# Sized transfer lengths in a planner, a second buffer for a reciprocal, and one buffer for norm2 and the output tiles

## The chip, the cores and the metric

The kernel runs on one core of a Trainium2 chip. The metric is the device time of one execution in microseconds. A core has five engines with their own instruction queues: PE (TensorE, matrix products; its weight loads are listed as PEld), DVE (VectorE), ACT (ScalarE), POOL (GpSimd) and SP, which here only issues transfers. Each engine works through its queue in order; semaphores hold an instruction back until what it needs is there.

## What is computed

The reference puts two layers behind each other, for 8 images of 192 channels and 64 x 64 pixels, all in float32.

```python
# layer 0: four scans over the image, one per direction
x = conv1x1(x, W_in)                            # 192 -> 384 channels
x = depthwise 3x3 convolution(x, W_dw) + b_dw
p = conv1x1(x, W_xd)                            # 16 channels
ws, Ls, Us, Ds = (conv1x1(p, w) for w in (W_w, W_l, W_u, W_d))
Gl, Gm, Gr = the three parts of ws, each / (|Gl| + |Gm| + |Gr| + 1e-7)
for 8 steps t:                                  # columns in chunks of 8
    h = l * x + gl * h_up + gm * h + gr * h_down
out = h * Us + xs * Ds                          # x, x transposed, both mirrored
y = sum over the 4 directions with w_m
y = layernorm over channels; global response norm over the image
y = conv1x1(y, W_out)                           # 384 -> 192
# layer 1: attention in windows of 8 x 8, then a two-layer network
s = layernorm(tokens); q, k, v = s @ qkv_w
a = normalised(q) . normalised(k) * temperature # 6 heads of 32
a = where(a >= 16th largest of its row, a, -100) + position bias
x2 = s + (softmax(a) @ v) @ proj_w
x2 = x2 + gelu(layernorm(x2) @ fc1_w) @ fc2_w
```

## The kernel before

Each image goes through three stages. `front` (lines 495 to 610) reads 8 image rows at a time, projects them on PE, writes them with a border to `pad` in HBM, reads strips of four rows back (three transfers for each strip, line 553), convolves them on PE (line 565) and writes the result twice to HBM, as `xs` and `xsT` (lines 598, 599). `scan` (from line 613) makes 8 steps t. A step loads `x0` (line 631), makes the 16-channel proxy `xe`, `xo`, and then 12 tiles of 128 channels x 512 pixels (4 directions x 3 channel tiles), each with a load `xd` for three of the directions (line 694). A tile takes four gate products on PE (line 678), absolute values on ACT (735, 757), products with the state on DVE (742, 744), sums on POOL (766, 781, 785), the sum of the absolute values on DVE (774), then a reciprocal as a logarithm and an exponential on ACT (777, 779) into the tile `rr`; `rr` is multiplied onto the sum on DVE (792) and onto the state products on POOL (796), and DVE makes the new state (800, 807). Pairs of tiles are added to the output `y3` (lines 833 to 855). `norm` (from line 861) normalises `y3` over the channels with the help of two small tiles, `m4` here and `xq` in the proxy, and stores it to `z` in HBM (line 928). `window_row` (from line 1009) treats 8 image rows, that is 8 windows: it loads `zg` (line 1032), scales it (1037), projects to tokens (1052), makes q, k, v (1102, 1141), the attention (1217 to 1332), the projection with the residual into `x2` (1366, 1378), the second norm into `xn` (1421), the network (1453, 1457, gelu 1473, 1487), and writes two output tiles: `ot0` (channels 0 to 127) and `ot1` (the other 64), made on ACT from PSUM (line 1501) and sent by SP (1513, 1516).

The order of all this is not the order of the program. Every operation is handed to a `Plan` as a step: its engine, its estimated cost, what it reads and writes, a rank, and a lane. `Plan.run` makes a list schedule from these estimates: of the steps whose inputs are ready and whose buffers are free by its own account, an engine takes the one of lowest rank, if it needn't idle over 40 ns for it. `Plan.order` does this twelve times with ranks corrected by the last schedule, keeps the shortest by its own estimates, and emits the instructions in that order. The engines then follow it at run time, with semaphores for the true dependences. A step's cost has two parts: how long it holds its engine, and how much later its result is there. For transfers, whose engine is SP, this was `dma(n)`: 350 ns for each of n transfers, and 2600 ns more.

Image b's scan is planned beside the window rows of image b - 1 and the front of image b + 1. So the kernel begins with the front of image 0 alone, then image 0's scan with the front of image 1, and ends with the rows of image 7 alone.

A tile that a `Held` names is made when the plan reaches its first user. Its tag and `bufs` say which buffers it shares and how many there are: the next tile of the tag gets a buffer when all users of an earlier one are done. An entry (tile, "room") makes a step on PE wait, in the plan, for that buffer, though the step itself doesn't write the tile. Before the change `rr` has one buffer, `ot0` shares the one of `xn`, `ot1` has its own, and `m4` and `xq` have one each.

Of the kernel before, what the change touches and what calls it, by code (L numbers as in the profile page):

```python
# [31 lines left out]
P = 128  # L32
B, DM, H, W = 8, 192, 64, 64
DIN, ND, NS = 384, 4, 16
CT = DIN // P
CH = 8
HEADS, HD, WS = 6, 32, 8
# [7 lines left out]
RG = 32  # L45
NEG = -100.0
# [242 lines left out]
def tile_ss2d_then_window_attention(ctx: ExitStack, tc: tile.TileContext, a: dict, out: bass.AP):  # L289
# [6 lines left out]
    nc = tc.nc  # L296
# [47 lines left out]

    ident = blank("ident", [P, P])
    make_identity(nc, ident)
    mean384 = blank("mean384", [P, P], 1.0 / DIN)
    eps5 = blank("eps5", [P, 1], 1e-5)
    eps7 = blank("eps7", [P, 1], 1e-7)
    neg = blank("neg", [P, 64], NEG)  # L350

    hid = [[blank(f"hid{d}_{ct}", [P, (H + 2) * CH], 0.0) for ct in range(CT)] for d in range(ND)]

# [109 lines left out]
    mm = lambda slots, n, share=1.0: (slots * n * 4.0, share)  # L463

    mg = lambda share=1.0: (512 * 5.0 + 240, share)
    dma = lambda n=1: (350.0 * n, 2600.0)
    tiny = (150.0, 90.0)
    log_c = {}
    log_half = blank("log_half", [P, 1], math.log(0.5) / 3)
# [25 lines left out]
    def front(b, xs, xsT):  # L495
        xb = x[b]
        padded = pad[b % 2]

        def read(s):


            def get():
                for k in range(2):
                    rows = slice(8 * (s + k), 8 * (s + k) + 8)
                    nc.sync.dma_start(xt[:, k], xb[0:P, rows, :])
                    nc.sync.dma_start(xt[64 * k : 64 * k + 64, 2], xb[P:DM, rows, :])

            plan("SP", dma(4), get, w=["xt", (xs, "room"), (xsT, "room")])

        def project(ct, s):  # L510

            own = padded[ct * P : (ct + 1) * P]
            cols = slice(ct * P, (ct + 1) * P)
            pins = [bank() for _ in range(2)]

            def products():
                outs = [p().rearrange("p (h w) -> p h w", h=8) for p in pins]
                for k in range(2):
                    nc.tensor.matmul(outs[k], lhsT=w_in[:, 0, cols], rhs=xt[:, k], start=True, stop=False)
                for k in range(2):  # L520
                    half = slice(64 * k, 64 * k + 64)
                    nc.tensor.matmul(outs[k], lhsT=w_in[half, 1, cols], rhs=xt[half, 2], start=False, stop=True)

            plan("PE", mm(3, 512), products, r=["xt"], w=pins)
            for k in range(2):
                cur, pin = xin[k], pins[k]
                plan(
                    "ACT",
                    act(512),
                    lambda cur=cur, pin=pin: nc.scalar.copy(  # L530
                        cur[:, :, 1 : W + 1], pin().rearrange("p (h w) -> p h w", h=8)
                    ),
                    r=[pin],
                    w=[("xin", k)],
                )
                plan(
                    "SP",
                    dma(),
                    lambda cur=cur, row=8 * (s + k) + 1: nc.sync.dma_start(own[:, row : row + 8, :], cur),
                    r=[("xin", k)],  # L540
                    w=[("pad", b % 2, ct, s + k)],
                )

        def convolve(ct, s):

            own = padded[ct * P : (ct + 1) * P]
            pc = bank()
            for k in range(2):
                strip = strips[k]

                def read(row=8 * s + 4 * k, strip=strip):
                    for dy in range(3):
                        nc.sync.dma_start(
                            strip[dy * RG : (dy + 1) * RG],
                            own[:, row + dy : row + dy + 4, :].rearrange("(q m) h w -> m q (h w)", m=RG),
                        )

                near = [("pad", b % 2, ct, n) for n in range(max(0, s + k - 1), min(NG, s + k + 1))]
                plan("SP", dma(3), read, r=near, w=[("strip", k)])
                rows4 = strip.rearrange("p q (h w) -> p q h w", h=4)  # L560

                def products(k=k, rows4=rows4):
                    for dx in range(3):
                        for q in range(4):
                            nc.tensor.matmul(  # L565
                                pc()[q * RG : (q + 1) * RG, k * 256 : (k + 1) * 256].rearrange("p (h w) -> p h w", h=4),
                                lhsT=w_cv[:, ct, q, dx, :],
                                rhs=rows4[:, q, :, dx : dx + W],
                                start=dx == 0,
                                stop=dx == 2,  # L570
                            )
# [16 lines left out]
            sn = Held(fpool, [P, 8, W], "sn")  # L588
            plan(
                "ACT",  # L590
                act(512),
                lambda: nc.scalar.activation(
                    sn(), pc().rearrange("p (h w) -> p h w", h=8), AF.Identity, bias=b_dw[:, ct : ct + 1]
                ),
                r=[pc],
                w=[sn],
            )
            plan("SP", dma(), lambda: nc.sync.dma_start(xs()[:, ct, :, rows], st()), r=[st], w=[(xs, ct, s)])
            plan("SP", dma(), lambda: nc.sync.dma_start(xsT()[:, ct, :, rows], sn()), r=[sn], w=[(xsT, ct, s)])
# [12 lines left out]

    def scan(b, xs, xsT, z, made):
# [14 lines left out]
        def proxy(t):  # L628

            x0 = Held(spool, [P, CT, 512], "x0", bufs=1)  # L630
            plan("SP", dma(), lambda: nc.sync.dma_start(x0(), xs()[:, :, t, :]), r=[xs], w=[x0])
            px = bank()

            def products():
# [47 lines left out]
        def tile_of(t, d, ct, xp, x0, y3, last):  # L682

            ch = d * DIN + ct * P
            if d == 0:
                xd = x0
                flat = lambda: x0()[:, ct, :]
            else:
                xd = Held(spool, [P, 512], "xd", bufs=4)
                src = xs if d == 2 else xsT  # L690
                plan(
                    "SP",
                    dma(),
                    lambda: nc.sync.dma_start(xd(), src()[:, ct, CH - 1 - t if d >= 2 else t, :]),
                    r=[(src, ct, s) for s in range(NG)],
                    w=[xd],
                )
                flat = lambda: xd()
# [71 lines left out]

            def rest():
                if t > 0:
                    rr = Held(spool, [P, 512], "rr", bufs=1)
                    plan("DVE", vec(512), lambda: nc.vector.tensor_add(nb(), nb(), ab()[:, 0, :]), r=[ab], w=[nb])  # L774

                    plan(
# [84 lines left out]
        def norm(t, y3):  # L861
            pm = bank()

            def means(dst, src):

                for ct in range(CT):
                    for q in range(4):
                        nc.tensor.matmul(
                            dst()[RG * q : RG * (q + 1), 0:P],
                            lhsT=mean384[:, 0:RG],  # L870
                            rhs=src()[:, ct, q * P : (q + 1) * P],
                            start=ct == 0,
                            stop=ct == CT - 1,
# [7 lines left out]
                        dst()[:, q * P : (q + 1) * P], lhsT=first, rhs=src(), start=True, stop=True  # L881
                    )

            m4 = Held(spool, [P, P], "m4", bufs=1)
            plan("PE", mm(3, P), lambda: means(pm, y3), r=[y3], w=[pm])
            plan("ACT", act(P), lambda: nc.scalar.copy(m4(), pm()[:, 0:P]), r=[pm], w=[m4])
            plan("PE", mm(4, P), lambda: spread(pm, m4), r=[m4], w=[pm])
# [37 lines left out]
                r=[pv],  # L925
                w=[y3],
            )
            plan("SP", dma(), lambda: nc.sync.dma_start(z()[:, :, t, :], y3()), r=[y3], w=[(z, t)])
            for ct in range(CT):
                plan(  # L930
                    "ACT",
# [52 lines left out]
        def mean_g():  # L984
            for ct in range(CT):
                nc.tensor.matmul(
                    pg()[:, 0:1], lhsT=mean384, rhs=gn()[:, ct : ct + 1], start=ct == 0, stop=ct == CT - 1
                )

        plan("PE", mm(3, 128), mean_g, r=[gn], w=[pg])  # L990
# [18 lines left out]
    def window_row(b, g, z, sc, bb):  # L1009
# [19 lines left out]


        zg = Held(lpool, [P, CT, CH, 64], "zg", bufs=1)
        plan("SP", dma(), lambda: nc.sync.dma_start(zg(), z()[:, :, :, g * 64 : (g + 1) * 64]), r=[z], w=[zg])

        def scaled_up():
            for ct in range(CT):
# [443 lines left out]
        for ci in range(2):  # L1479
            pf = bank()  # L1480
            n = GT // (ci + 1)

            ot = Held(lpool, [P, WS, n // WS], f"ot{ci}", bufs=1, tag="ot1" if ci else "xn")
            def narrowed(ci=ci, pf=pf, n=n):
                def sums(lhsT, rhs, at, k, **flags):
                    dst = pf()[64 * k : 64 * k + 64] if ci else pf()
# [145 lines left out]
```

## Time and profile before

| what | value |
|---|---|
| three runs | 8303.1, 8295.51, 8274.17 us (median 8295.51) |
| profiled execution | 8293.82 us |
| span of its instructions | 8292.0 us |
| mean granted clock of PE | 0.827 |
| busy: PE, DVE, POOL, ACT | 6951.0, 6381.9, 5859.7, 5488.0 us |
| moved by DMA | 695.70 MB, 84 GB/s over the span |
| convolution of the strips (565, PE) | 9216 matmuls, 678.3 us busy |
| logarithm, exponential into rr (777, 779) | 672 each, mean 685 and 633 ns |
| multiplications by rr (792 DVE, 796 POOL) | 672 each, mean 692 and 1298 ns |

Busy time is the time in which an engine executes, as a share of the span. The profile also cuts the span in 40 slices with the busy tenths of each engine. A group of instructions has its busy time, the mean of one, and the idle time of its engine just before it with what ended it ("<-"). A line of the waits names the waiting engine and line, what ended the wait, the total, the number and the longest. The windows view gives the busy times within chosen stretches.

### The profile page before, as it was taken

How to read it: one execution, taken by the hardware profiler on the slowest of the kernel's cores; microseconds unless marked ns; L12 is line 12 of the kernel's file. 1: busy time of each engine (PE TensorE's matmuls, PEld its weight loads, DVE VectorE, ACT ScalarE, POOL GpSimd, SP SyncE). 2: the span in 40 equal slices, each digit the busy share in tenths (PEclk: the TensorE clock that was granted, in tenths of full speed). 3: DMA queues.
4: the chain of work that ended last, by engine and by line, in shares of the span. 5: the costliest groups of instructions: out<-in, count | busy, mean ns of one | idle time of the engine just before them, and what ended most of it. 6: DMA issues, size and time to landing. Idle time of an engine off the chain costs nothing.

```text
span 8292.0 us, 147108 instructions
## 1 busy us (share of the span) xinstructions
PE 6951.0 (84%) x51224; PEld 3600.7 (43%) x51224; DVE 6381.9 (77%) x15421; ACT 5488.0 (66%) x12537; POOL 5859.7 (71%) x5918
## 2 busy tenths in 40 slices
PE   5677688788988898888988898888888789888887
PEld 2333344444444444444444444444444444444454
DVE  1366777888788987888788887888888888888643
ACT  1355346766677666777577766777677676677787
POOL 0377877788778877788778777778788788877411
PEclk8887579788898788888898889888788887778898
DMA  6776146111542135411532126311111112111110
GB/s 175 193 191 180 42 128 165 50 44 45 139 129 74 52 96 138 107 45 56 157 103 77 46 76 171 91 46 46 57 41 50 43 41 66 41 48 41 30 22 15
DMA packets 1037948, 695.70 MB, mean 84 GB/s; under 512 B 704115, under 2 KB 860214, under 8 KB 1037206
## 3 DMA queue, kind: packets, MB, share of 16 engines
q1 hardware_dynamic: 1035830, 684.99, 30.9%
q8 instruction: 407, 6.67, 0.3%
q14 instruction: 335, 2.74, 0.1%
q10 hardware_dynamic: 1376, 1.30, 0.1%
HBM read 453.43 MB, written 232.67 MB: 83 GB/s over the span
## 4 chain that ended last, share of the span: by engine, by line
PE 23%; ACT 15%; DVE 14%; POOL 9%; DMA 5%; issue 4%; SPq 0%; POOLq 0%; DVEq 0%; ACTq 0%
PE g L678 6%; PE lp L1487 3%; PE lp L1453 2%; ACT at L1286 2%; ACT at L1298 2%; DMA zg<-z 2%; POOL pr L796 2%; PE lp L1052 2%; PE lp L565 2%; DVE pr L742 1%; PE lp L1102 1%; POOL pr L781 1%; ACT ab L735 1%; DMA strip<-pad 1%; POOL ab L766 1%
## 5 line engine op out<-in xcount | busy, mean ns | idle before, releaser
L678 PE MATMUL g<-xe,w_g 32*128 32x512 f32 x3648 | 1281.3, 777 | 284.0 <-DVE dx L833 90.3
L678 PE MATMUL g<-xo,w_g 32*128 32x512 f32 x3648 | 1218.2, 767 | 270.1 <-DVE dx L833 154.0
L796 POOL TENSOR_TENSOR pr<-pr,rr 128x512 f32<-128x512 f32 x672 | 872.5, 1298 | 369.4 <-ACT rr L779 320.5
L781 POOL TENSOR_TENSOR pr<-pr 128x512 f32<-128x512 f32 x672 | 887.2, 1321 | 339.7 <-DVE pr L742 254.8
L766 POOL TENSOR_TENSOR ab<-ab 128x512 f32<-128x512 f32 x672 | 873.4, 1300 | 269.6 <-ACT ab L735 264.7
L735 ACT ACTIVATE ab<-g 128x512 f32<-128x512 f32 x1344 | 778.7, 594 | 295.1 <-PE nb L678 175.5
L847 POOL TENSOR_TENSOR dx<-dx,hu 128x512 f32<-128x512 f32 x576 | 738.8, 1294 | 257.6 <-DVE hu L838 250.8
L565 PE MATMUL lp<-strip,w_cv 128*32 128x256 f32 x9216 | 678.3, 438 | 289.0 <-DMA strip<-pad 265.9
L785 POOL TENSOR_TENSOR pr<-pr 128x512 f32<-128x512 f32 x672 | 884.2, 1316 | 20.6
L678 PEld LDWEIGHTS g<-xe,w_g 32*128 32x128 f32 x3648 | 451.9, 219 | 835.0 <-DVE dx L833 206.5
L678 PEld LDWEIGHTS g<-xo,w_g 32*128 32x128 f32 x3648 | 423.4, 217 | 812.4 <-DVE dx L833 278.4
L777 ACT ACTIVATE rr<-nb,eps 128x512 f32<-128x512 f32 x672 | 460.4, 685 | 436.5 <-DVE nb L774 320.8
L1487 PE MATMUL lp<-hd,w_f 128*64 128x256 f32 (+1 forms) x2304 | 610.1, 505 | 63.4 <-ACT hd L1473 39.7
L792 DVE SCALAR_TENSOR_TENSOR nb<-nb,rr 128x512 f32<-128x512 f32 x672 | 464.7, 692 | 237.6 <-ACT rr L779 236.1
L565 PEld LDWEIGHTS lp<-strip,w_cv 128*32 128x32 f32 x9216 | 313.5, 122 | 659.3 <-issue 388.6
L855 POOL TENSOR_TENSOR y<-y,dx 128x512 f32<-128x512 f32 x384 | 593.9, 1555 | 1.8
L800 DVE SCALAR_TENSOR_TENSOR nb<-nb,pr 128x512 f32<-128x512 f32 x672 | 464.4, 691 | 152.5 <-POOL pr L796 148.1
L774 DVE TENSOR_TENSOR nb<-nb,ab 128x512 f32<-128x512 f32 x672 | 464.7, 691 | 128.9 <-POOL ab L766 98.8
L845 POOL TENSOR_TENSOR y<-hu,dx 128x512 f32<-128x512 f32 x192 | 247.3, 1296 | 418.8 <-DVE hu L838 415.7
L757 ACT ACTIVATE nb<-nb 128x512 f32<-128x512 f32 x672 | 397.8, 592 | 206.5 <-DVE pr L742 107.8
L838 DVE TENSOR_TENSOR hu<-g,hid 128x512 f32<-128x512 f32 x768 | 511.4, 678 | 4.6 <-PE g L678 1.7
L678 PE MATMUL nb<-xe,w_g 32*128 32x512 f32 x672 | 506.4, 844 | 8.8 <-DVE hid L807 8.6
(202 smaller groups left out, 17104.4 us busy)
## 6 DMA issues: line engine op xcount, KB each, us to landing
strip<-pad SPq DMA_DIRECT2D x1152, 132.0 KB
xd<-xsT SPq DMA_DIRECT2D x384, 256.0 KB
pad<-xin SPq DMA_DIRECT2D x192, 264.0 KB
xs<-st SPq DMA_DIRECT2D x192, 256.0 KB
xsT<-sn SPq DMA_DIRECT2D x192, 256.0 KB
xd<-xs SPq DMA_DIRECT2D x192, 256.0 KB
x<-xs SPq DMA_DIRECT2D x64, 768.0 KB
z<-y SPq DMA_DIRECT2D x64, 768.0 KB
```

Source lines behind the costliest of these rows:

```text
L565: nc.tensor.matmul(pc()[q * RG : (q + 1) * RG, k * 256 : (k + 1) * 256].rearrange("p (h w) -> p h w", h=4), lhsT=w_cv[:, ct, q, dx, :], rh ...
L678: nc.tensor.matmul(dst, lhsT=w[rows, col : col + P], rhs=xp[rows, :], start=True, stop=True)
L735: lambda r=r: nc.scalar.activation(ab()[:, r, :], g[r](), AF.Abs),
L766: plan("POOL", gp(512), lambda: nc.gpsimd.tensor_add(ab()[:, 0, :], ab()[:, 0, :], ab()[:, 1, :]), w=[ab])
L774: plan("DVE", vec(512), lambda: nc.vector.tensor_add(nb(), nb(), ab()[:, 0, :]), r=[ab], w=[nb])
L781: plan("POOL", gp(512), lambda: nc.gpsimd.tensor_add(one(), one(), pr()[:, 1, :]), r=[(pr, 1)], w=[(pr, 0)])
L785: lambda: nc.gpsimd.tensor_add(one(), one(), pr()[:, 2, :]),
L796: plan("POOL", gp(512), lambda: nc.gpsimd.tensor_mul(one(), one(), rr()), r=[rr], w=[(pr, 0)])
L838: lambda: nc.vector.tensor_mul(like(hu(), d), like(pu(), d), state(d, ct)),
L847: plan("POOL", gp(512), lambda: nc.gpsimd.tensor_add(dx(), dx(), hu()), r=[hu], w=[dx])
L855: nc.gpsimd.tensor_add(y, y, dx().rearrange("p (c i) -> p i c", c=CH))
L1487: nc.tensor.matmul(dst[:, at : at + rhs.shape[-1]], lhsT=lhsT, rhs=rhs, **flags)
```

## The change

Three things are edited. The estimate of a transfer's hold on SP takes its size: `dma(n, kb)` holds for the larger of 350 ns for each transfer and 5.4 ns for each KB of the step; the part for the landing stays at 2600 ns. Ten calls are given their KB; those of the small `flat` and of `xe` stay without. `rr` gets a second buffer. `ot1` moves into the buffer of `xn`, which `ot0` already uses, `m4` moves into that of `xq`, and two constants shrink: `mean384` from 128 to 32 columns, whose first column one small product (line 986) now takes broadcast, and `neg` from 64 columns to one. No instruction of the computation is added or taken away; the planner's order is computed anew.

```diff
-    mean384 = blank("mean384", [P, P], 1.0 / DIN)
+    mean384 = blank("mean384", [P, RG], 1.0 / DIN)
...
-    neg = blank("neg", [P, 64], NEG)
+    neg = blank("neg", [P, 1], NEG)
...
-    dma = lambda n=1: (350.0 * n, 2600.0)
+    dma = lambda n=1, kb=0: (max(350.0 * n, 5.4 * kb), 2600.0)
...
-            plan("SP", dma(4), get, w=["xt", (xs, "room"), (xsT, "room")])
+            plan("SP", dma(4, 786), get, w=["xt", (xs, "room"), (xsT, "room")])
...
-                plan("SP", dma(3), read, r=near, w=[("strip", k)])
+                plan("SP", dma(3, 396), read, r=near, w=[("strip", k)])
...
-            plan("SP", dma(), lambda: nc.sync.dma_start(xs()[:, ct, :, rows], st()), r=[st], w=[(xs, ct, s)])
+            plan("SP", dma(1, 360), lambda: nc.sync.dma_start(xs()[:, ct, :, rows], st()), r=[st], w=[(xs, ct, s)])
...
-            plan("SP", dma(), lambda: nc.sync.dma_start(x0(), xs()[:, :, t, :]), r=[xs], w=[x0])
+            plan("SP", dma(1, 768), lambda: nc.sync.dma_start(x0(), xs()[:, :, t, :]), r=[xs], w=[x0])
...
-                    rr = Held(spool, [P, 512], "rr", bufs=1)
+                    rr = Held(spool, [P, 512], "rr", bufs=2)
...
-            m4 = Held(spool, [P, P], "m4", bufs=1)
+            m4 = Held(spool, [P, P], "m4", tag="xq", bufs=1)
...
-                    pg()[:, 0:1], lhsT=mean384, rhs=gn()[:, ct : ct + 1], start=ct == 0, stop=ct == CT - 1
+                    pg()[:, 0:1], lhsT=mean384[:, 0:1].to_broadcast([P, P]), rhs=gn()[:, ct : ct + 1], start=ct == 0, stop=ct == CT - 1
...
-        plan("SP", dma(), lambda: nc.sync.dma_start(zg(), z()[:, :, :, g * 64 : (g + 1) * 64]), r=[z], w=[zg])
+        plan("SP", dma(1, 900), lambda: nc.sync.dma_start(zg(), z()[:, :, :, g * 64 : (g + 1) * 64]), r=[z], w=[zg])
...
-            ot = Held(lpool, [P, WS, n // WS], f"ot{ci}", bufs=1, tag="ot1" if ci else "xn")
+            ot = Held(lpool, [P, WS, n // WS], f"ot{ci}", bufs=1, tag="xn")
...
-            plan("SP", dma(1 + ci), put, r=[ot], w=[("out", b, g, ci)])
+            plan("SP", dma(1 + ci, 256 >> ci), put, r=[ot], w=[("out", b, g, ci)])
```

The other transfers get their sizes in the same way: the write of `pad` 264, `xsT` 360, `xd` 256, `z` 768.

More of the change, by code (lines that the diff above doesn't have):

```diff
@@ L537, in project @@
                     "SP",
-                    dma(),
+                    dma(1, 264),
                     lambda cur=cur, row=8 * (s + k) + 1: nc.sync.dma_start(own[:, row : row + 8, :], cur),
@@ L597, in convolve @@
             )
-            plan("SP", dma(), lambda: nc.sync.dma_start(xs()[:, ct, :, rows], st()), r=[st], w=[(xs, ct, s)])
-            plan("SP", dma(), lambda: nc.sync.dma_start(xsT()[:, ct, :, rows], sn()), r=[sn], w=[(xsT, ct, s)])
+            plan("SP", dma(1, 360), lambda: nc.sync.dma_start(xs()[:, ct, :, rows], st()), r=[st], w=[(xs, ct, s)])
+            plan("SP", dma(1, 360), lambda: nc.sync.dma_start(xsT()[:, ct, :, rows], sn()), r=[sn], w=[(xsT, ct, s)])
         for s in range(0, NG + 1, 2):
@@ L692, in tile_of @@
                     "SP",
-                    dma(),
+                    dma(1, 256),
                     lambda: nc.sync.dma_start(xd(), src()[:, ct, CH - 1 - t if d >= 2 else t, :]),
@@ L869, in means @@
                             dst()[RG * q : RG * (q + 1), 0:P],
-                            lhsT=mean384[:, 0:RG],
+                            lhsT=mean384,
                             rhs=src()[:, ct, q * P : (q + 1) * P],
@@ L927, in norm @@
             )
-            plan("SP", dma(), lambda: nc.sync.dma_start(z()[:, :, t, :], y3()), r=[y3], w=[(z, t)])
+            plan("SP", dma(1, 768), lambda: nc.sync.dma_start(z()[:, :, t, :], y3()), r=[y3], w=[(z, t)])
             for ct in range(CT):
```

## Prediction

> **What bounds the kernel now.** I read the busy shares by slice first, then the scan's steps one by one, then the waits, then single stretches of the timeline.
>
> ```profile
> PE 6951.0 (84%) x51224; PEld 3600.7 (43%) x51224; DVE 6381.9 (77%) x15421; ACT 5488.0 (66%) x12537; POOL 5859.7 (71%) x5918
> ...
> PE   5677688788988898888988898888888789888887
> ...
> POOL 0377877788778877788778777778788788877411
> PEclk8887579788898788888898889888788887778898
> DMA  6776146111542135411532126311111112111110
> ```
>
> No engine is full throughout, so it is a kernel of regimes. In the first four slices DMA is the busiest (0.6 to 0.7). From 860 to 7550 us a window of the trace gives PE 5740.6 and DVE 5577.0 of 6690 us (86% and 83%), POOL 78%: three engines near their limit, tied by a fixed order. In the last three slices, where only window rows remain, POOL falls to 0.1 to 0.4.
>
> Image 0's scan runs alone with the front of image 1. Its steps lie between successive loads of x (line 631); the columns are PE, PEld, DVE, ACT, POOL busy with their instructions, PE clock, DMA share and GB/s:
>
> ```profile
> 390.20:512.50 122.30, 94.41 (x904) 41.41 (x902) 80.50 (x128) 67.71 (x112) 89.11 (x71) 0.89 0.82 216
> 512.50:633.80 121.30, 91.96 (x726) 39.93 (x728) 79.48 (x127) 60.91 (x106) 88.27 (x71) 0.80 0.68 179
> 633.80:748.50 114.70, 93.51 (x848) 40.54 (x837) 76.81 (x121) 63.59 (x105) 84.80 (x67) 0.85 0.79 208
> 748.50:859.70 111.20, 74.92 (x471) 35.39 (x472) 78.53 (x124) 48.13 (x85) 86.36 (x70) 0.66 0.39 101
> 859.70:962.20 102.50, 67.54 (x234) 33.61 (x233) 78.93 (x125) 40.50 (x73) 86.66 (x70) 0.52 0.14 42
> ```
>
> POOL does the same 85 to 89 us each time, yet a step takes 102.5 us without front work and up to 122.3 with it. The waits of 860 to 7550 us tell what stops an engine:
>
> ```profile
> POOL pr L796 <- ACT rr L779: 282.2, 161, 11.2
> DVE nb L792 <- ACT rr L779: 200.1, 162, 7.7
> ...
> ACT rr L777 <- POOL pr L796: 88.5, 41, 5.7
> ACT zg L1037 <- DMA zg<-z: 82.7, 30, 7.4
> PE lp L565 <- DMA strip<-pad: 82.6, 40, 6.6
> PE lp L638 <- DMA x<-xs: 48.2, 23, 4.1
> ```
>
> Columns: total, times, longest. The third line is the single rr buffer; the last three are engines that reached an instruction before its transfer had landed. One case of the rr buffer:
>
> ```profile
> 904.23 0.70 DVE L774 TENSOR_TENSOR nb<-nb,ab 128x512 f32<-128x512 f32 x1 [0.86 <-POOL ab L766]
> 905.35 1.29 POOL L796 TENSOR_TENSOR pr<-pr,rr 128x512 f32<-128x512 f32 x1
> ...
> 906.67 0.69 ACT L777 ACTIVATE rr<-nb,eps 128x512 f32<-128x512 f32 x1 [4.04 <-POOL pr L796]
> ```
>
> The sum was ready at 904.93; the logarithm began at 906.67, when POOL had read rr: 1.7 us late.
>
> **What the Trainium skill says.** "Perfetto Trace Analysis", Optimization Strategy: with several regimes, interleave them. The table above agrees that front work is bunched in three steps; no run yet shows that spreading pays. "DMA: Bandwidth & Descriptors", Specifications: transfers need 512 bytes for the full rate. Here 704115 of 1037948 packets are smaller and the fullest step moved 216 GB/s; the trace agrees in direction only. "TensorE: Matmul & The Clock Gate", Part 1: an idle PE falls to half clock. Agrees: 0.52 granted at 66% busy in the last step shown.
>
> **The change, part by part.** Against the profiled execution: 8293.82 us, a span of 8292.0 with 1.8 around it, 1.7 under the median of 8295.51.
>
> *Lengths of transfers.* No transfer is added; the planner now counts more, and orders all five engines anew. Before, it counted a load of x as 0.35 + 2.6 = 2.95 us; among the longest pieces of the chain of waits "DMA x<-xs" stands with 4.9 to 7.5 us and "DMA zg<-z" with 5.4 to 8.5. Now x counts 768 x 5.4 ns + 2.6 = 6.7 us, zg 7.5, three strips 4.7 instead of 3.65. PE and ACT work behind a transfer is put later, and SP's whole queue is laid out by bandwidth. From the SP order of both kernels, times the KB of the page's sixth part, the MB issued in image 0's seven steps (from its second load of x at 313.3 us to image 1's first at 1065.4) are 15.5, 25.7, 20.9, 23.7, 9.9, 4.2, 4.2 before and 12.5, 17.5, 16.1, 15.3, 18.9, 17.2, 6.0 after: the same total, spread. Before the first load of x it stays (43.3 and 43.0 MB), so the start of the scan at 270 us stays.
>
> (A) Image 0. Over 102.5 us, the four heavy steps cost 19.8 + 18.8 + 12.2 + 8.7 = 59.5 us. If only bunching cost, all of it goes. But the excess is nearly proportional to MB (8.7 us at 9.9 MB, 19.8 at 25.7), which says that the work itself costs, wherever it stands: then nothing goes. In its favour, 270 to 860 us holds 90.1 us of PE waiting for strips with scan matmuls queued behind it. I take half: -30; bounds -60 and 0.
>
> (B) 860 to 7550 us. PE waits for strips 82.6, x 48.2 and xe 23.5 (the same list, further down), 154 us in all. What is late next is DVE at 83%, so a freed PE gains only in part. I take a quarter: -38; bounds -77 (half) and 0. ACT's 82.7 us for zg I count at nothing: ACT is 69% busy there and hides it.
>
> *Second rr buffer.* It removes no instruction. In the ACT order 144 of 672 logarithms wait for POOL before and none after; in the DVE order, however, only 19 of 672 tiles form their sum (L774) before the tile ahead has been divided (L792), so the planner hardly uses it. (C) Of the 88.5 us a quarter, since the engine that waits is ACT: -22; bounds -88 and 0.
>
> *Shared output buffer.* xn, ot0 and ot1 now pass through one buffer. ot1's activation (ACT, line 1501) must wait for ot0's transfer to land; behind it on ACT stand the next rows' copies, for which PE waits. At the end of the kernel ot0's transfer is issued at 8285.47 and ot1's activation starts at 8287.48. A 64 KB transfer took 2.5 us (last issue ended 8289.5, end 8292.0), the 264 KB pad write 3.6 to 4.2 in the chain, so ot0 (256 KB) lands 8288.0 to 8289.7: +0.5 to +2.2, taken +1.3. In the last eight rows the planner also holds the next projection back until ot1 has landed. Those rows' ot0 activations run from 7936.7 to 8284.3, a pitch of 49.7 us; the row's own cycle (projection 8249.8 to ot1's landing 8292.0) is 42.2, plus the wait for ot0, some 4.4, makes 46.6: it just fits. I take 1 us a row: (D) 1.3 + 8 = +9; bounds 0 and +72 (9 us for each row). In mid-kernel a row has about 118 us (the first x load of image 1 at 1065.4 us, of image 7 at 6753.2: 948 an image, 8 rows), which covers it.
>
> (E) m4 in xq's buffer: each is used once a step, far apart; hidden by the 100 us between, 0 (if they met, a 3 us delay on a side lane). The broadcast constants: 24 matmuls at L986 (weight loads of L880, broadcast too, take 214 to 223 ns against 206 of plain ones at L1102: under 1 us) and 192 predicated copies of 1227 ns; the row of L891, with a broadcast operand, is no slower per element (1750 / 1536) than plain ones (691 / 512), so 0, bounds of 10% either way, 24 us on DVE.
>
> (F) After the last scan matmul the PE order leaves 9 rows' front halves and 11 rows' last matmuls instead of 8 and 10. Per row, PE spends 5.3 us on L1052, 1.4 on L1017, 6.6 on L1102, 3.4 on L1141 and 11.2 on L1487 (group sums over 64): 28 us moved from the scan into the tail; given back nearly whole: +5; bounds 0 and +28.
>
> Sum: -30 - 38 - 22 + 9 + 5 = -76, so 8218 profiled, 8220 against the median.
>
> **The rivals.** *More:* the order was what held the steady stretch, and all waits at their bounds go: -60 - 77 - 88 = -225, 8070. For: 282 + 200 us of POOL and DVE stand behind rr. Against: the 19 of 672. *Nothing:* cost follows MB, and each wait is replaced by one on DVE or POOL: A, B, C near 0, D and F +14, 8305. For: the proportion in the steps. *Slower:* one mechanism, the row's cycle in the tail. With 9 us whole in each of eight rows (+72), the 28 us of moved work on top, and A to C at a third (-30): +70, 8364. It decides once the pitch exceeds the 49.7 us of now by more than the gain before, about 11 us a row. For: xn, ot0, ot1 and x are one ring. Against: 46.6 is under 49.7, and in the new PE order the attention of the next row stands between the two halves of the last-but-one output.
>
> **How the numbers follow.** Likeliest case 0.56 (8165 to 8268), more 0.17, nothing 0.15, slower 0.12. A difference of under 0.3% (25 us) can't be told from no change. Faster 0.73, same 0.15, slower 0.12. From 8100, most of the way to the large gain, to 8315, past the case of nothing: some 0.18 is left out.
>
> **What would show it.** A: the steps that took 122, 121, 115 and 111 us come near 105 to 110. B: the strip and x lines under the waits fall by half. C: "ACT rr L777 <- POOL pr L796" vanishes. D: ot1's activation waits on a DMA 1 to 3 us; tail pitch 50 to 51 us. It is wrong if the seven steps still sum to 752 us (313.3 to 1065.4), if waits on DVE grow as those on DMA fall, or if the tail grows by over 30 us.

## The result and the profile after

The changed kernel takes 8047.48 us (median of three runs, 8045.24 to 8055.83) against 8295.51 before: a ratio of 0.9709, 95% interval 0.9692 to 0.9726. That is 248 us less, where 76 were forecast, and below the range.

The page of the changed kernel, its busy shares and PE's slices:

```profile
PE 6996.1 (87%) x51224; PEld 3590.4 (45%) x51224; DVE 6296.7 (78%) x15421; ACT 5494.0 (68%) x12537; POOL 5821.2 (72%) x5918
...
PE   5788788888998899889999899988988898888887
```

The instruction counts of these engines are equal. DVE's busy time fell by 85 us (from 6381.9), POOL's by 39, PE's rose by 45. The slices of PE with an 8 or 9 went from 32 to 36, and the share of PE rose from 84% to 87%: idle time went. The mean granted clock rose from 0.827 to 0.838, but as PE's busy time did not fall, faster matmuls are not the gain. Cut at the loads of x, the spans of the two profiled executions (8292.0 and 8045.7 us) differ so:

| stretch | before | after | difference |
|---|---|---|---|
| start to the first x load | 270.6 | 260.5 | -10 |
| first to second x load | 42.7 | 36.8 | -6 |
| image 0's seven steps | 752.1 | 705.3 | -47 |
| middle: image 1's first x load to image 7's | 5687.8 | 5471.5 | -216 |
| image 7's first to its last x load | 797.2 | 771.3 | -26 |
| last x load to the end | 741.7 | 800.4 | +59 |

The steps of image 0 that took 122, 121, 115, 111 and 102.5 us, in the windows view of after (columns as in the prediction):

```profile
375.10:480.80 105.70, 87.41 (x627) 35.79 (x620) 79.65 (x125) 57.07 (x98) 87.70 (x71) 0.82 0.66 170
480.80:580.10 99.30, 86.63 (x635) 35.40 (x632) 78.24 (x125) 55.80 (x94) 88.45 (x70) 0.81 0.65 168
580.10:682.70 102.60, 87.08 (x534) 33.70 (x534) 78.79 (x126) 51.60 (x90) 88.00 (x71) 0.79 0.56 153
682.70:791.10 108.40, 94.06 (x676) 38.31 (x674) 78.99 (x125) 59.13 (x103) 85.86 (x68) 0.82 0.69 180
791.10:899.30 108.20, 91.80 (x641) 38.69 (x640) 78.94 (x125) 55.04 (x96) 87.25 (x70) 0.77 0.61 158
```

POOL's 86 to 88 us are as before, the front's transfers now run at an even 153 to 180 GB/s, and a step takes hardly longer than the 102.5 us without front work. The waits of after between 790 and 7245 us, the same part of the program as 860 to 7550 before:

```profile
POOL pr L796 <- ACT rr L779: 238.2, 141, 9.8
...
DVE nb L792 <- ACT rr L779: 216.4, 167, 4.3
...
POOL ab L766 <- ACT ab L735: 130.3, 101, 11.3
...
PE g L678 <- DMA xe<-flat: 13.8, 5, 4.4
...
PE lp L565 <- DMA strip<-pad: 9.9, 10, 1.9
...
ACT zg L1037 <- DMA zg<-z: 5.8, 4, 2.1
```

Of before, the prediction shows all of these but one transfer and POOL's wait for absolute values (219.3 us); the transfer is

```profile
PE g L678 <- DMA xe<-flat: 23.5, 6, 7.1
```

PE's idle time for transfers fell from 154 us (82.6 + 48.2 + 23.5) to 24, ACT's for zg from 82.7 to 6. The line for rr on ACT is gone. POOL's wait for absolute values from ACT fell from 219.3 us to 130.3, perhaps because ACT's queue stalls less in front of them; no run separates this. The two lines of POOL and DVE behind rr sum to 455 us, against 482.

One group's form changed as well. The groups of before and of after, kept apart by shape (busy time, mean of one in ns, idle time before):

```profile
L1261 DVE COPY_PREDICATED at<-less,neg 128x512 f32<-128x512 uint8 x192 | 235.5, 1227 | 6.6
```

```profile
L1261 DVE COPY_PREDICATED_SCALAR at<-less,neg 128x512 f32 x192 | 152.3, 793 | 6.8
```

With `neg` of one column the predicated copy is another operation, and takes 793 ns instead of 1227: 83 us of DVE, which is nearly the whole of its 85.

### The profile page after: what moved, and what is told of

Same layout as the page of the kernel before. It is cut to its first block, busy times and chain, and to the rows that moved or that the text cites. A ratio compares the mean times of both kernels' runs of the same rounds, so it can differ in the third digit from the quotient of the medians.

```text
span 8045.7 us, 146948 instructions
## 1 busy us (share of the span) xinstructions
PE 6996.1 (87%) x51224; PEld 3590.4 (45%) x51224; DVE 6296.7 (78%) x15421; ACT 5494.0 (68%) x12537; POOL 5821.2 (72%) x5918
## 4 chain that ended last, share of the span: by engine, by line
PE 21%; ACT 16%; DVE 12%; POOL 11%; issue 3%; DMA 1%; SPq 0%; POOLq 0%; DVEq 0%; ACTq 0%
PE g L678 6%; PE lp L1487 3%; ACT at L1298 2%; PE lp L1453 2%; ACT at L1286 2%; POOL pr L796 2%; POOL ab L766 2%; POOL pr L781 2%; POOL pr L785 1%; PE lp L1102 1%; POOL dx L847 1%; ACT hd L1473 1%; PE lp L565 1%; ACT ab L735 1%; PE lp L1457 1%
## 5 line engine op out<-in xcount | busy, mean ns | idle before, releaser
L678 PE MATMUL g<-xe,w_g 32*128 32x512 f32 x3648 | 1302.8, 772 | 261.7 <-DVE dx L833 86.5
L678 PE MATMUL g<-xo,w_g 32*128 32x512 f32 x3648 | 1229.7, 747 | 210.3 <-DVE dx L833 98.0
L781 POOL TENSOR_TENSOR pr<-pr 128x512 f32<-128x512 f32 x672 | 880.2, 1310 | 316.7 <-DVE pr L742 238.8
L785 POOL TENSOR_TENSOR pr<-pr 128x512 f32<-128x512 f32 x672 | 871.2, 1297 | 22.2
L678 PEld LDWEIGHTS g<-xe,w_g 32*128 32x128 f32 x3648 | 456.9, 216 | 831.9 <-DVE dx L833 197.1
L678 PEld LDWEIGHTS g<-xo,w_g 32*128 32x128 f32 x3648 | 425.7, 211 | 754.7 <-DVE dx L833 223.8
L678 PE MATMUL nb<-xe,w_g 32*128 32x512 f32 x672 | 515.8, 860 | 6.9 <-DVE hid L807 6.9
```

The costliest lines, as they stand in the source:

```text
L678: nc.tensor.matmul(dst, lhsT=w[rows, col : col + P], rhs=xp[rows, :], start=True, stop=True)
L781: plan("POOL", gp(512), lambda: nc.gpsimd.tensor_add(one(), one(), pr()[:, 1, :]), r=[(pr, 1)], w=[(pr, 0)])
L785: lambda: nc.gpsimd.tensor_add(one(), one(), pr()[:, 2, :]),
```

## The experiments

Theory W: the sizes did it, because in the planner's fixed order a wait that it had not counted is not hidden, on whichever engine. Rivals: the second rr buffer did half or more; or the effect is the luck of another order; a third is the cheaper predicated copy. Theory D: the shared output buffer is what lengthened the tail. Each kernel was profiled once and timed in three rounds (the last two in five) beside the kernel before, whose median was 8277 to 8296 us in the five sets. The ratio is to it.

| kernel | sizes | rr | neg | ot1 in | time, us | ratio (interval) | middle | W: PE + ACT | tail | pitch |
|---|---|---|---|---|---|---|---|---|---|---|
| before | none | 1 | 64 | own | 8295.5 | | 5687.8 | 151 + 86 | 742 | 49.7 |
| n_before_360 | none (360 ns) | 1 | 64 | own | 8253.9 | 0.997 (0.9958-0.9983) | 5662.7 | 103 + 91 | 722 | 49.8 |
| e2_buffers_only | none | 2 | 1 | xn | 8348.3 | 1.0074 (1.0057-1.009) | 5699.3 | 112 + 106 | 799 | 57.1 |
| e9_ot1_shared | none | 1 | 64 | xn | 8370.4 | 1.0088 (1.0068-1.0108) | 5688.7 | 119 + 90 | 820 | 55.2 |
| e10_zg_size | zg | 1 | 64 | own | 8218.6 | 0.993 (0.9903-0.9957) | 5612.6 | 106 + 16 | 744 | 48.5 |
| e11_zg_size_360 | zg (360 ns) | 1 | 64 | own | 8165.4 | 0.9867 (0.984-0.9895) | 5542.6 | 103 + 15 | 761 | 52.5 |
| e6_front_sizes | front | 2 | 1 | xn | 8192.4 | 0.9902 (0.9887-0.9917) | 5583.8 | 80 + 74 | 826 | 57.9 |
| e7_rest_sizes | all but front | 2 | 1 | xn | 8151.9 | 0.9858 (0.984-0.9876) | 5527.3 | 80 + 15 | 800 | 54.1 |
| e5_landing | as landing | 2 | 1 | xn | 8124.9 | 0.9807 (0.9791-0.9823) | 5511.9 | 89 + 17 | 780 | 54.0 |
| after | all | 2 | 1 | xn | 8047.5 | 0.9709 (0.9692-0.9726) | 5471.5 | 24 + 8 | 800 | 53.7 |
| c_5_6 | all (5.6) | 2 | 1 | xn | 8054.2 | 0.9733 (0.9719-0.9748) | 5452.2 | 24 + 6 | 816 | 56.1 |
| e1_sizes_only | all | 1 | 1 | own | 8055.0 | 0.9724 (0.9709-0.974) | 5518.5 | 22 + 4 | 774 | 51.7 |
| e1_sizes_5_6 | all (5.6) | 1 | 1 | own | 7999.2 | 0.9638 (0.9624-0.9653) | 5473.9 | 18 + 0 | 746 | 52.2 |
| e3_one_rr | all | 1 | 1 | xn | 7995.1 | 0.9651 (0.9637-0.9666) | 5446.7 | 20 + 9 | 767 | 55.8 |
| e3_one_rr_5_6 | all (5.6) | 1 | 1 | xn | 8075.6 | 0.9726 (0.9707-0.9745) | 5486.2 | 27 + 2 | 814 | 57.2 |
| e8_m4_shared | all | 1 | 1 | own | 8065.2 | 0.9719 (0.9704-0.9735) | 5522.0 | 32 + 6 | 779 | 52.1 |
| e12_ot1_in_sq | all | 2 | 1 | sq | 8018.0 | 0.9683 (0.9653-0.9713) | 5475.0 | 32 + 10 | 737 | 49.8 |
| e13_ot1_in_sq_5_6 | all (5.6) | 2 | 1 | sq | 7996.0 | 0.966 (0.9633-0.9687) | 5476.6 | 14 + 10 | 737 | 51.3 |
| e14_sizes_neg64 | all | 1 | 64 | own | 8093.0 | 0.9765 (0.975-0.978) | 5551.1 | 28 + 10 | 775 | 51.7 |
| e15_before_neg1 | none | 1 | 1 | own | 8243.2 | 0.9938 (0.9924-0.9952) | 5637.5 | 141 + 86 | 739 | 49.6 |

Middle is the stretch of the table above; W is the idle time of PE and of ACT that a landing transfer ended, from image 0's last x load to image 7's; tail runs from the last x load to the end; pitch is the mean distance of the last eight ot0 activations. These four are of the profiled execution. neg is its number of columns; every kernel but before, n_before_360, e9, e10, e11 and e15 also has the narrow `mean384`, which no pair takes apart.

The ten kernels with all sizes lie between 7995 and 8093 us, the five with none between 8243 and 8370. The scatter between orders, which the controls below put at up to 81 us, doesn't bridge the 150 us between the groups: the sizes are a cause of the gain, and luck is not enough for it.

**One half of the change at a time.** e1 is the kernel before with the sized `dma`, its ten sizes and the narrow constants, that is the changed kernel with

```diff
-                    rr = Held(spool, [P, 512], "rr", bufs=2)
+                    rr = Held(spool, [P, 512], "rr", bufs=1)
...
-            m4 = Held(spool, [P, P], "m4", tag="xq", bufs=1)
+            m4 = Held(spool, [P, P], "m4", bufs=1)
...
-            ot = Held(lpool, [P, WS, n // WS], f"ot{ci}", bufs=1, tag="xn")
+            ot = Held(lpool, [P, WS, n // WS], f"ot{ci}", bufs=1, tag="ot1" if ci else "xn")
```

e2 is the changed kernel with

```diff
-    dma = lambda n=1, kb=0: (max(350.0 * n, 5.4 * kb), 2600.0)
+    dma = lambda n=1, kb=0: (350.0 * n, 2600.0)
```

> The kernel before with the sized transfer lengths alone: one rr buffer, ot1 and m4 in buffers of their own. Theory 1 (the lengths made the gain: in the steady stretch PE's waits for transfers fell from 154 to 24 us and each freed microsecond counted in full): 8060 to 8110 us, PE's waits for strips and x between 860 and 7550 us under 40 us. Rival (the second rr buffer made half or more of the gain, since ACT's 88 us for it vanished and POOL's wait for absolute values fell by 89): 8170 to 8250 us.

> The changed kernel with the old estimate of transfers (350 ns each whatever the size), so only the buffers differ from before. Theory 1: within 40 us of the kernel before (8255 to 8335 us), with PE's waits for strips, x and xe still near 150 us. Rival (rr makes half or more of the gain): 8170 us or less.

e1 gives 8055.0 (5 us under its range), as fast as the changed kernel, with one rr buffer: the rival of rr falls. (Both kernels have the narrow constants too, so the buffers are not all that sets e2 apart from before; the last pair takes neg apart.) e2 gives 8348.3, some 60 us worse than before. e2 was expected within 40 us of before and is outside; its middle (5699.3) is that of before, its tail 57 us longer. Against e15 below, which has the same narrow neg, e2 is 105 us slower.

**One rr buffer in the changed kernel.**

```diff
-                    rr = Held(spool, [P, 512], "rr", bufs=2)
+                    rr = Held(spool, [P, 512], "rr", bufs=1)
```

> The changed kernel with one rr buffer; ot1 and m4 stay shared, lengths stay sized. Theory 1: 8050 to 8110 us. If sharing xn's buffer cost the tail its 59 us, this run stands above the run with the lengths alone by 30 to 60 us, and its last eight rows keep a pitch near 54 us; if the longer tail comes only from one more row left over, the two are within 20 us and the pitch is the same in both.

7995.1, below what was expected and 52 us under the changed kernel, with a shared output buffer. Neither branch about the tail fits the total: it lies 60 us under e1, not above, though the pitch is 55.8 against e1's 51.7. The two controls were made to tell whether such a number means anything.

**Controls.** One estimate is altered by 3 or 4%, and nothing else, in the changed kernel and in the kernel before:

```diff
-    dma = lambda n=1, kb=0: (max(350.0 * n, 5.4 * kb), 2600.0)
+    dma = lambda n=1, kb=0: (max(350.0 * n, 5.6 * kb), 2600.0)
```

```diff
-    dma = lambda n=1: (350.0 * n, 2600.0)
+    dma = lambda n=1: (360.0 * n, 2600.0)
```

> A control: the changed kernel with 5.6 instead of 5.4 ns for each KB, a difference of 4% in one estimate that tells the planner nothing new. If the planner's orders vary little by chance, 8030 to 8065 us. If they scatter by tens of us for no reason, differences such as the 60 us between the two kernels with one rr buffer (8055 with own, 7995 with shared output buffers) are no evidence about the buffers; then this run is 30 us or more away from 8047.

> A second control: the kernel before with 360 instead of 350 ns for each transfer. Little scatter: 8270 to 8305 us. Scatter of tens of us: 30 us or more from 8288.

The changed kernel at 5.6 is 7 us away; the kernel before at 360 is 23 us away from its set's 8276.9 (34 from the 8288 that the expectation names). To test e3, the first of these edits was made in e1 and in e3 as well:

> The kernel with the lengths alone, at 5.6 instead of 5.4 ns for each KB. It tells the scatter at this place: within 15 us of 8055 if the gap to 7995 is of the buffers, 8000 to 8040 if the gap is scatter.

> Sized lengths at 5.6, one rr, shared output buffers. If the second rr buffer does harm (8047 and 8054 with two against 7995 with one), 7980 to 8015 us again. If 7995 was a lucky order, 8030 to 8070.

They turned round: 7999.2 with own buffers, 8075.6 with shared ones and one rr. The order's luck moves a kernel by 7, 23, 56 and 81 us in these four pairs (and by 53 and 22 between e10 and e11, e12 and e13). A single difference under some 80 us between two orders is therefore no evidence here; e3's 7995.1 was a lucky order.

**Hold or landing.** The size is put in the landing instead of SP's hold:

```diff
-    dma = lambda n=1, kb=0: (max(350.0 * n, 5.4 * kb), 2600.0)
+    dma = lambda n=1, kb=0: (350.0 * n, 2600.0 + max(0.0, 5.4 * kb - 350.0 * n))
```

> The changed kernel with the size counted as a later landing only: SP is held 350 ns for each transfer as before, and the landing is put later by what the size adds. Theory 1a (what mattered is that PE and ACT work is put behind the true landing): 8040 to 8110 us, PE's waits for transfers under 50 us in the steady stretch. Theory 1b (what mattered is that SP's queue has a bandwidth, so that front work is spread): 8180 to 8260 us, and the transfers of image 0's steps are bunched as before (over 20 MB in three steps).

8124.9, between the two expectations, and the stretches tell why. Image 0's steps stay bunched, as the windows view of this kernel shows for its third to seventh step:

```profile
376.20:497.20 121.00, 97.65 (x856) 42.08 (x858) 80.81 (x128) 67.11 (x113) 89.51 (x72) 0.86 0.80 205
...
617.50:727.70 110.20, 92.62 (x827) 40.72 (x828) 75.39 (x119) 62.01 (x103) 84.84 (x68) 0.90 0.86 220
727.70:842.30 114.60, 85.95 (x684) 37.98 (x684) 78.91 (x125) 57.91 (x98) 86.75 (x69) 0.76 0.61 154
842.30:944.00 101.70, 71.00 (x235) 34.13 (x232) 79.20 (x125) 40.80 (x74) 86.77 (x70) 0.52 0.15 42
```

The seven steps sum to 741 us, against 751 in e2 and 705 with the hold. The middle falls from e2's 5699.3 to 5511.9, 187 of the 228 us that the hold brings. So the spreading in image 0 needs the hold on SP's queue; most of the middle's gain seems to need only that work stands behind the true landing (one order each).

**Which transfers.** e6 keeps the sizes of the front's transfers alone; e7 those of all others. In the changed kernel, e6 and then e7 (the other calls alike):

```diff
-                    dma(1, 256),
+                    dma(),
...
-            plan("SP", dma(1, 768), lambda: nc.sync.dma_start(x0(), xs()[:, :, t, :]), r=[xs], w=[x0])
+            plan("SP", dma(), lambda: nc.sync.dma_start(x0(), xs()[:, :, t, :]), r=[xs], w=[x0])
```

```diff
-                plan("SP", dma(3, 396), read, r=near, w=[("strip", k)])
+                plan("SP", dma(3), read, r=near, w=[("strip", k)])
```

> The changed kernel with sizes only for the transfers of the front (image rows, pad, strips, xs, xsT); x, xd, z, zg and the output tiles count 350 ns each as before. Of the 240 us that the sizes are worth (all sizes, 8045, against buffers alone, 8348, is even 300), theory F (the front's queue is what was mis-planned: strips late, three steps bunched) gives 8050 to 8130 us and image 0's seven steps near 700 us. Rival R (the loads of x and zg, with 5 us each on the way, matter as much) gives 8180 to 8260.

> The complement: sizes only for x, xd, z, zg and the output tiles, the front at 350 ns each. Theory F: 8270 to 8350 us, with PE's waits for strips as in the kernel with the buffers alone and image 0's seven steps near 750 us. Rival R: 8130 to 8230, ACT's waits for zg near 10 us instead of 106.

8192.4 and 8151.9 both fall in the ranges of rival R: the loads of x and zg matter as much as the front. Theory F is right only about image 0, whose seven steps take 692 us in e6 and 724 in e7. Each half alone is worth more than half (156 and 196 us under e2; together 301), so the two gains overlap. The waits of the middle in e6, from 770 to 7364 us, and in e7, from 800 to 7344:

```profile
ACT zg L1037 <- DMA zg<-z: 71.9, 32, 5.5
...
PE lp L565 <- DMA strip<-pad: 56.4, 22, 5.7
```

```profile
PE lp L565 <- DMA strip<-pad: 66.2, 35, 4.3
...
ACT zg L1037 <- DMA zg<-z: 8.5, 5, 3.7
```

With zg unsized ACT waits for it, with the strips unsized PE waits for them: what is late in each kernel is what was counted too short there, though with the strips sized PE still waits 56.4 us for them in e6.

**zg alone.** The kernel before, with a size for one transfer (e10; in e11 350 is 360 as well):

```diff
-    dma = lambda n=1: (350.0 * n, 2600.0)
+    dma = lambda n=1, kb=0: (max(350.0 * n, 5.4 * kb), 2600.0)
...
-        plan("SP", dma(), lambda: nc.sync.dma_start(zg(), z()[:, :, :, g * 64 : (g + 1) * 64]), r=[z], w=[zg])
+        plan("SP", dma(1, 900), lambda: nc.sync.dma_start(zg(), z()[:, :, :, g * 64 : (g + 1) * 64]), r=[z], w=[zg])
```

> The kernel before with a size for zg alone (900 KB, at 5.4 ns). Theory W (in the middle stretch a wait for a transfer costs its full length, on ACT as on PE): ACT's waits for zg fall from 86 us to under 15, the span by 60 to 110 us, 8170 to 8235 us. Rival (ACT at 69% hides it): 8250 to 8300.

> The same at 360 ns for each transfer, to be set against the kernel before at 360 (8254). Theory W: 8150 to 8200 us. Rival: 8240 to 8290.

e10 is 65 us under its set's 8284.0, e11 is 89 under the 8253.9 of another set: both in the ranges of theory W. The waits of e10 from 860 to 7486 us:

```profile
PE lp L638 <- DMA x<-xs: 46.0, 20, 5.5
...
PE lp L565 <- DMA strip<-pad: 45.0, 28, 5.7
...
ACT zg L1037 <- DMA zg<-z: 7.3, 7, 2.5
```

ACT's wait went from 86 to 16 us (the W column) while PE's wait for x stayed (46.0 against 48.2). The middle fell by 75 and 120 us. In e10 PE's waits fell as well (151 to 106); at 360 they did not (103 to 103), so there they are not the gain. Two things stay open: 65 us is within the scatter of orders, and so is a part of 89; and the size of zg also holds SP longer, which these runs don't separate from ACT's wait (in e11 the middle fell by more than the 76 us that ACT's wait lost).

**Where ot1 lies.** e9 is the kernel before with ot1 in xn's buffer and nothing else; e8 has all sizes, one rr, m4 in xq's buffer and ot1 in its own; e12 and, at 5.6, e13 are the changed kernel with ot1 in the buffer of `sq`, which a row uses early. The line of e9, of e8 against e3, and of e12:

```diff
-            ot = Held(lpool, [P, WS, n // WS], f"ot{ci}", bufs=1, tag="ot1" if ci else "xn")
+            ot = Held(lpool, [P, WS, n // WS], f"ot{ci}", bufs=1, tag="xn")
```

```diff
-            ot = Held(lpool, [P, WS, n // WS], f"ot{ci}", bufs=1, tag="xn")
+            ot = Held(lpool, [P, WS, n // WS], f"ot{ci}", bufs=1, tag="ot1" if ci else "xn")
```

```diff
-            ot = Held(lpool, [P, WS, n // WS], f"ot{ci}", bufs=1, tag="xn")
+            ot = Held(lpool, [P, WS, n // WS], f"ot{ci}", bufs=1, tag="sq" if ci else "xn")
```

> The kernel before with one edit: ot1 in xn's buffer (lengths unsized, one rr). In the kernels so far the last eight rows have a pitch of 49.7 to 51.7 us where ot1 has its own buffer and 53.7 to 57.9 where it shares. Theory D (the ring xn, ot0, ot1 costs the tail): 8300 to 8350 us, pitch 54 us or more. Rival (the longer tail is the planner's scatter): 8255 to 8300 us, pitch near 50.

> Sized lengths, one rr, m4 sharing with xq, but ot1 in its own buffer: between the kernel with the lengths alone (8055, both own) and the one with both shared (7995). Theory D: the tail's pitch falls to 50 to 52 us, and the run is at or under 7995 (7940 to 7995). Rival (the 60 us between those two are scatter, or ot1's sharing helps mid-kernel): 8020 to 8070.

> The changed kernel, two rr buffers, but ot1 shares the buffer of sq (the squares of q and k, used early in a row and briefly) instead of xn's. Theory D+: the tail's pitch is 50 to 52.5 us instead of 53.7 and the tail 30 to 50 us shorter, 7990 to 8025 us. If the second rr buffer helps in the middle, the middle stretch (5471 us) stays and the total is under 7999. Rival (sq's buffer makes a new ring): 8047 or more.

> The same at 5.6 ns for each KB, against 8054. Theory D+: 7990 to 8030 us, pitch 50 to 52.5 us.

e9 gives 8370.4, above even the expectation, with a pitch of 55.2. e8's pitch is 52.1, at the edge of what was expected, but its total, 8065.2, is in the rival's range, that of scatter: its middle is 5522, at the high end of the sized ones. e12 and e13 give 8018.0 and 7996.0, pitch 49.8 and 51.3, as expected; their tails are 63 and 79 us shorter than with xn's buffer, more than expected. Over all 20 profiles the nine with ot1 in xn's buffer have pitches of 53.7 to 57.9 us and tails of 767 to 826 (mean 802); the eleven others 48.5 to 52.5 and 722 to 779 (mean 751). The pitches don't overlap. The tails do, and not all of their difference is the ring's: eight of the nine have 13 ot0 activations after the last x load, but only six of the eleven. Among those with 13 the means are 807 and 762 us, with 12 they are 767 (one kernel) and 737, so the ring itself costs some 30 to 45 us, and the row left over some 25 to 40. Whether the ring also makes the planner leave that row over, as happened in e9 (13 instead of 12), is open. How the ring works shows in one row of the tail of the changed kernel:

```profile
7661.59 1.11 ACT L1501 ACTIVATE ot<-lp,b_f 128x512 f32<-128x512 f32 x1
...
7662.72 0.34 SPq L1513 DMA_DIRECT2D out_dram<-ot  x1
...
7668.93 2.81 PE L1487 MATMUL lp<-hd,w_f 128*64 128x256 f32 x24
...
7672.22 0.72 ACT L1501 ACTIVATE ot<-lp,b_f 128x256 f32<-128x256 f32 x1 [1.66 <-PE lp L1487]
```

and in one of the kernel before, where the second half follows the first at once:

```profile
8142.60 1.14 ACT L1501 ACTIVATE ot<-lp,b_f 128x512 f32<-128x512 f32 x1
...
8144.54 0.71 ACT L1501 ACTIVATE ot<-lp,b_f 128x256 f32<-128x256 f32 x1
```

The two activations stand 10.6 us apart instead of 1.9. The (ot, "room") entry makes the planner hold ot1's products back until, by its account, ot0 has landed, and the next row's projection (L1366), which waits for room for xn, until ot1 has. In the other rows it is the same: of the last eight, all but the very last have 7.5 to 10.6 us between the two activations, and 6.5 to 10.1 in e9, against 1.7 to 3.3 before and 1.5 to 6.5 in e12.

**neg of one column.** Only the constant is altered; the planner doesn't see it. In the traces of each pair the orders of DVE, ACT, POOL and SP are the same to the instruction, and PE's but for neighbouring gate products that run at the same time, so no luck of an order is in these two. In e1 (giving e14), and turned round in the kernel before (giving e15):

```diff
-    neg = blank("neg", [P, 1], NEG)
+    neg = blank("neg", [P, 64], NEG)
```

> The kernel with the sizes alone, but neg with 64 columns as before, in the same order. The predicated copies take 83 us more of DVE. If DVE's time counts in full: 8138 us. If half of it: 8097. If DVE hides it: 8055 to 8070. Theory W alone makes the gain only if this run stays near 8055.

> The kernel before with neg of one column, in the same order. In full 8205 to 8215 us; half 8250; hidden 8275 to 8295.

e14 gives 8093.0, 38 us over e1 (of another set); e15 8243.2, 49 us under the kernel before in the same set (8292.3). Both are the case of half: of 75 to 83 us of DVE, some 40 to 50 are seen in the time. So e1's gain was not of the sizes alone, and neither was that of the changed kernel.

## Why the prediction was wrong

The side was right, the size not: 248 us instead of 76. Step by step:

- **A (image 0), -30 forecast, -47 measured** (and -16 before those steps, which was not forecast). The near proportion of excess to MB was read as half an argument that the work itself costs. For the most part it didn't: with 15 to 19 MB a step, the excess over 102.5 us is 3.2 - 3.2 + 0.1 + 5.9 + 5.7 = 12 us, of 59.5 before. The proportion was read off two steps; the step with 23.7 MB had cost only 12.2 us. e5 speaks for SP's hold as what brought the gain, and the seven steps of all kernels agree: 689 to 708 us where the front's sizes are held, 724 to 759 where they aren't.
- **B (middle), -38 forecast: this is the term that failed most.** The waits were rightly found, and they fell as described, PE's by 131 us (154.3 to 23.7) and ACT's by 77. Two factors of the term were wrong: "I take a quarter", since DVE would be late next, and "ACT's 82.7 us for zg I count at nothing". Over the 20 profiles a line by least squares gives middle = 5452 + 0.89 x W + 35 for the wide neg, with 28 us of scatter about it and a standard error of 0.09 on the factor: where a microsecond of W goes, about one goes from the middle, not a quarter. The line compares kernels with and without sizes; within the five without and within the ten with all, W varies too little to give a factor (0.2 and 0.5, with standard errors over 1). So whatever else the sizes did to the order is in the factor too, and that the waits themselves cost their full length is the reading that fits, not shown apart. How the factor divides between PE and ACT the 20 profiles don't settle (0.4 and 1.4, each with a standard error of about 0.25). That ACT's part isn't nothing, e10 and e11 speak for: a size for zg alone lowered the middle by 75 and 120 us. From before to after W falls by 205 us; with the 35 the line makes that 217, and 216 were measured (these two profiles are among the 20).
- **E (constants), 0 forecast with 24 us either way: it failed too.** "The row of L891, with a broadcast operand, is no slower per element" looked only for a loss in the same operation; the narrow operand made it another one, 35% shorter. e14 and e15 put 38 and 49 us to it. A freed microsecond of DVE, 83% busy, was thus worth about half of itself.
- **C (second rr buffer), -22 forecast; no effect can be told from the scatter.** ACT's wait for the buffer vanished as forecast. But e1 at 5.6 keeps 96 us of it and has a middle of 5473.9, while the four fully sized kernels with two buffers have 5452 to 5477. Against the five with one (5447 to 5522, all with the narrow neg) their mean is 21 us lower, as much as was forecast, but the spread of the five is 75, so it shows neither the 22 nor nothing. The trace of after bears out the 19 of 672 sums. A wait that the planner counts is one round which it has put other work; one that it doesn't know stands in front of work which it believed to be running. This reading fits both numbers, and was not tested by itself.
- **D and F (tail), +14 forecast, +59 measured.** The bounds held it. "46.6: it just fits" compared the row's cycle with the mean pitch as though the planner could fill every gap: the pitch rose from 49.7 to 53.7, which over the seven distances is 29 us. e9 and e12 put this down to ot1's place. The other 30 us stand before the first of the last eight ot0 activations, where one row more is left over, as F had it (12 of them before, 13 after); F took +5, with 28 as its bound. The wait of ot1's activation on the last row, taken as 1.3 us, was about 0.2 (8040.93 to 8041.14): the transfer of 256 KB landed in some 2 us.

Of the rivals, "more" came within 23 us of the result for a wrong reason: it put 88 us on rr, which gave nothing near that, and left out zg and the constant, so it was luck. "It is wrong if the tail grows by over 30 us" came true, hidden under the larger gain. Four slips change nothing: in the fourth slice DMA (6 tenths) was behind PE and POOL (7), "nothing" sums to 8308, not 8305, and in the chain the shortest piece of zg is 5.6 us, not 5.4, the longest write of pad 4.6, not 4.2.

In sum, by size: the sized lengths some 200 us (e14 against before: 199, of two different orders, so with their scatter), the narrow `neg` 40 to 50, the second rr buffer nothing that can be told from the scatter, and the room is paid for by a tail some 30 to 60 us longer. These sum to some 200, not 248; most of the rest lies in the middle of the changed kernel (80 us shorter than e14's, 33 to 50 of them neg's) and is within what the order's luck moves. In totals the price of the shared buffer is clearest without sizes (e9 74 us over before, e2 105 over e15); with sizes and one rr buffer it is lost in the scatter (7995 and 8076 shared, 8055 and 7999 own), and with two the sign is the same but each difference is under the scatter (8047 and 8054 in xn's buffer, 8018 and 7996 in sq's). The fastest kernels, 7995 to 7999, beat both given ones; which of them is best the scatter doesn't say.

## What to carry to other kernels

Where a planner fixes the order of every engine, look for the waits that it did not count: here the time fell by about the whole length of the idle gaps that ended with a landing transfer, and sizing one that only ACT, 69% busy, waited for lowered it by 65 and 89 us; the cure was a true duration in the plan. Compare the operations by name before and after, not only their counts: a smaller constant changed one into a cheaper one. Before a difference between two planned orders is put down to an edit, alter one estimate by a few per cent and see how far the time moves by itself (7 to 81 us here). Freeing room by closing buffers to a ring has a price where nothing else can fill the gap, at the end of the kernel.

## What was not expected of the hardware

A predicated copy of 128 x 512 from a constant takes 793 ns when the constant is one column for all (the trace then calls it COPY_PREDICATED_SCALAR), and 1188 to 1227 ns when it is 64 columns repeated, 192 times in each profile.

The strips' matmuls cost image 0's steps little time once spread (108.2 us against 102.5), though PE's busy time rose from 67.5 to 92 us in the step that had none before: the granted clock of that step rose from 0.52 to 0.77. The Trainium skill ("TensorE: Matmul & The Clock Gate", Part 1) says that idleness halves the clock, and the 0.52 agrees. Here the reverse was of use: the strips' 31.9 us of PE were partly paid for by the faster clock, as the gate products (L678) of that step took 45.9 us instead of 59.0.
